# A graph network on one core: pre_u and pre_v from products of their own, and where VectorE's scoring stands in two units

## The chip, the cores and the metric

The kernel runs on one core of a Trainium2 chip. The metric is the device time of one launch in microseconds (us). The engines are TensorE (PE, with its weight loads shown as PEld), VectorE (DVE), ScalarE (ACT), GpSimd (POOL) and SyncE (SP). Each takes its own instructions in order. POOL and SP here mainly issue DMAs.

## The reference

64 graphs of 256 nodes with 256 features pass through four layers; `adj` (256x256, about 3% of its entries set, the same for all graphs) is shared. Three layers (L0, L1, L3) are alike; L2 is an attention layer.

```
pre_u = h @ W1[:d];  pre_v = h @ W1[d:]
hidden = relu(pre_u[:, :, None, :] + pre_v[:, None, :, :] + b1)
S   = sigmoid(hidden @ W2 + b2)              # one score for each edge (u, v)
a_t = einsum('buv,bud->bvd', S * A, h)
m_t = einsum('uv,bud->bvd', A, h) * h
z   = beta1*h + beta2*(a_t @ Wa + ba) + beta3*(m_t @ Wm + bm)
```

Scores are needed only where `adj` is not zero. All numbers are float32.

## The kernel before

**Pairs and units.** Graphs go two at a time (a pair, index g). Two pairs, side "a" and side "b", run interleaved. One round takes both pairs through all layers, and there are 16 rounds, written out one after another. A *unit* is the scoring of one side's pair in one of the layers L0, L1, L3, with the other side's remaining stages issued beside it. The order in a round is a/L0, b/L0, a/L1, b/L1, a/L3, b/L3. `beside(heavy, light, placed)` (L911) interleaves them: `heavy` is the scoring, `light` a generator of small steps that yields how many steps of scoring come next, a number for `made` or a pair for (`made`, `got`). `STEPS` (L45) and the list `beside` in `before` (L656) hold these numbers.

**Stages of a side.** `before(st, l)` (L646) computes pre_u and pre_v, adds b1, writes them to two DRAM tables, and prepares the first rows of `pre`. `scores` (L700) rates the edges, `spread` (L865) puts the scores into `sa`, and `finish` (L368) makes `a_t` and z. For L3 `attention` (L425) comes first. `mixed` (L334) makes `m_t`. In the pre_u/pre_v part, node blocks have the index m (128 nodes each).

**Scoring.** An edge block (128 edges, both graphs) is made in one of two ways. `made` picks rows with a matmul from `pre` into PSUM (`ga<-pre,pick`); the needed rows of `pre` are copied on ACT by `rows_u` and `rows_v`. `got` takes blocks that POOL has gathered from the tables by indirect DMA (`fetch`, L814): first u, then v added to it. A unit has 18 such DMAs (22 in b/L1 and a/L3): f = 0 to 7 (9), each with a u and a v part, and one "left" block (f = -1). In `FETCHES` the last five of 18 are v of f=4, u of 7, v of 5, v of 6, v of 7. All go through POOL's queue in order; the first AHEAD = 6 are issued within `before`, the others when the unit starts. DVE rates each block with two instructions (`junk<-ga`, `junk<-fetched`, one for each graph), which leave sums in `raw`. `rated_all` turns these into scores: ACT `val<-raw`, `val<-val`, and four DVE `rm<-gva,val`. EARLY covers the left block, the diagonal and all blocks of edge half m = 0 (f = 0 to 3 and made blocks 0 to 3), LATE (16 columns, at the end of a unit) those of m = 1. After EARLY comes `early` (L849): `ro` on ACT, PE `ps<-ro,guo`, four DVE `sa<-diag,val,ps`.

**The end of a unit.** `spread` is the first work of the next unit: 16 matmuls `ps<-rm,gu` (32 records in the trace) in two halves, m = 0 on EARLY's `rm` and m = 1 on LATE's, and a DVE `sa<-sa,ps` after each. The next unit's first `ga` matmul stands in their neighbourhood and needs `pre` row 0.

**Placed or not.** With `placed` true, `made`, the diagonal and the fetched blocks are held where the plan puts them (`stay` pins an instruction behind the last one of its engine), and EARLY comes in mid-unit after at least four made blocks. With `placed` false nothing is pinned, EARLY waits for all made blocks, and the framework's scheduler orders each engine's queue by readiness. Before, `placed` is true except beside the attention (b/L1, a/L3) and in the first and last unit: L892 gives true for L1, L893 false for L3, and L891 `i > 0` for both sides' L0; the flag comes from the light stream. So the b/L3 unit, beside a's last layer and a's next L0 `before`, has it true.

**pre_u and pre_v before** (L667 to L695). For each of the four (m, g) one 512-wide product writes u and v side by side into one PSUM bank; ACT copies the u half to `pu`, DVE adds b1 to the v half into `pv`. For L0 and L3 a third instruction adds u (from PSUM) and `pv` into `own`. After g = 1 of a block m the two table writes go to SP's queue, and after the one of m = 0 the first fetches. For L3 the order is g outer, because h of graph 1 is ready later. Two PSUM pools hold 5 banks (`ps`) and 3 banks (`ga`).

Of the kernel before, what the change touches and what calls it, by code (L numbers as in the profile page):

```python
# [12 lines left out]
ALU = mybir.AluOpType  # L13
AX = mybir.AxisListType

P = 128
B, N, D = 64, 256, 256
GNN = ("L0_gnn_", "L1_gnn_", "L3_gnn_")
LAST = GNN[2]
# [19 lines left out]
FETCHES = [(0, 0), (1, 0), (2, 0), (0, 1), (3, 0), (1, 1)]  # L39
FETCHES += [(-1, 0), (2, 1), (4, 0), (3, 1), (-1, 1), (5, 0), (6, 0), (4, 1), (7, 0), (5, 1), (6, 1), (7, 1)]  # L40
FETCHES_MORE = FETCHES[:-2] + [(8, 0), (6, 1), (9, 0), (7, 1), (8, 1), (9, 1)]
# [3 lines left out]
STEPS = {  # L45
    GNN[0]: [(1, 1), (1, 1), (0, 1), (1, 0), (0, 1), (2, 1)],
    GNN[1]: [0, 0, 0, (0, 1), (0, 1), 1],
    LAST: [1, (1, 1), 0, (1, 1), (0, 1), (2, 1)],
}

VEC = {}
# [11 lines left out]
def blk(c):  # L63
    return slice(c * P, (c + 1) * P)
# [37 lines left out]
def adj_seq_kernel(ctx: ExitStack, tc: tile.TileContext, a: dict, out: bass.AP):  # L102
# [187 lines left out]
    def stages(pools):  # L290
# [62 lines left out]
        def kept(st, l):  # L353

            hb = one.tile([P, 2, 2, N], FP, tag="hb", name="hb")
            for i in range(2):
                if l == LAST:
                    for m in range(2):
                        vector.scalar_tensor_tensor(
                            hb[:, i, m, :], st["h"][i][:, m, :], sca(l + "beta1"), zbrow, ALU.mult, ALU.add  # L360
                        )
                else:
                    scalar.activation(
                        hb[:, i], st["hT"][:, i], AF.Identity, bias=zbias[l][:, i : i + 1], scale=sca(l + "beta1")
                    )
            return hb

        def finish(st, l):  # L368

            sa, mT = st["sa"], st["mT"]  # L370
            hb = kept(st, l)
            aT = one.tile([P, 2, 2, N], FP, tag="aT", name="aT")
            for g in range(2):
                t = psum()
                product(t, st["h"][g], sa[:, :, g, :])
                scalar.copy(aT[:, :, g, :], t)
                yield STEPS[l][g]
            if l == LAST:
                for g in range(2):
                    z = psum()  # L380
                    for m in range(2):
                        for j, (w, y) in enumerate(((wm[l], mT), (wa[l], aT))):
                            for c in range(2):
                                mm(out=z[:, m, :], lhsT=y[:, c, g, blk(m)], rhs=w[:, c, :],
                                   start=j == 0 and c == 0, stop=j == 1 and c == 1)
                        yield STEPS[l][2 + 2 * g + m]
                    o = h_tile(st, g)
                    vector.tensor_tensor(o, hb[:, g], z, ALU.add)
                    nc.sync.dma_start(
                        out=of_graph(out, st["b"] + g), in_=o  # L390
                    )
                return
            hT = hT_tile(st)
            for m in range(2):
                z = psum()
                for j, (w, y) in enumerate(((wm[l], mT), (wa[l], aT))):
                    for c in range(2):
                        mm(out=z, lhsT=w[:, c, blk(m)], rhs=y[:, c], start=j == 0 and c == 0, stop=j == 1 and c == 1)
                    if j == 0:
                        yield STEPS[l][2 + 2 * m]  # L400
                vector.tensor_tensor(hT[:, m], hb[:, m], z, ALU.add)
                yield STEPS[l][3 + 2 * m]
            st["hT"] = hT
            st["h"] = []

            def turn(g):
                t = psum()
                flip(t, hT[:, :, g, :])
                h = h_tile(st, g)
                if l == GNN[1]:  # L410

                    vector.tensor_tensor(h, t, bias2.unsqueeze(1).to_broadcast([P, 2, D]), ALU.add)
                else:
                    scalar.copy(h, t)
                st["h"].append(h)

            if l == GNN[1]:
                for g in range(2):
                    turn(g)
                    yield 0  # L420
            else:

                st["turn"] = turn
# [78 lines left out]
    def few(stack):  # L502
# [139 lines left out]
        def more(st, l):  # L642

            return (st["side"], l) in (("a", LAST), ("b", GNN[1]))

        def before(st, l):  # L646

            hT = st["hT"]
            pu = one.tile([P, 2, 2, D], FP, tag="pu" + st["side"], name="pu")
            pv = one.tile([P, 2, 2, D], FP, tag="pv" + st["side"], name="pv")  # L650
            pre = one.tile([P, len(FAST), 2 * D], FP, tag="pre" + st["side"], name="pre")
            order = [(m, g) for m in range(2) for g in range(2)]
            if l == LAST:
                order = [(m, g) for g in range(2) for m in range(2)]

            beside = {LAST: [0, (0, 1), (0, 1), (0, 1)], GNN[1]: [0] + [(0, 1)] * 3, GNN[0]: [(0, 1)] * 4}[l]  # L656
            beside = dict(zip(order, beside))
            st["tables"] = [
                tables.tile([N, 2 * D], FP, tag="table" + t + st["side"], name="table" + t) for t in "uv"
            ]  # L660

            st["pu"], st["pv"], st["pre"] = pu, pv, pre
            if l != GNN[1]:
                st["own"] = one.tile([P, 2, 2, D], FP, tag="own", name="own")
            t = one.tile([P, FIRST, 2, D], FP, tag="fetched" + st["side"], name="fetched")
            st["fetched"] = [t[:, f] for f in range(FIRST)]
            for m, g in order:  # L667
                if l == LAST and (m, g) == (1, 0):
                    st["flip"](1)
                t = psum()  # L670
                for c in range(2):
                    mm(out=t, lhsT=hT[:, c, g, blk(m)], rhs=w1[l][:, c], start=c == 0, stop=c == 1)
                scalar.copy(pu[:, m, g, :], t[:, 0, :])
                vector.tensor_tensor(pv[:, m, g, :], t[:, 1, :], b1row[l], ALU.add)
                if g == 1:
                    for rows, x in zip(st["tables"], (pu, pv)):
                        nc.sync.dma_start(out=rows[blk(m)], in_=flat(x)[:, m])
                    if m == 0:
                        st["fetches"] = list(FETCHES_MORE if more(st, l) else FETCHES)

                        if numbered:
                            fetch(st, AHEAD)
                if l != GNN[1]:
                    vector.tensor_tensor(st["own"][:, m, g, :], t[:, 0, :], pv[:, m, g, :], ALU.add)
                if g == 1:
                    if m == 0:
                        rows_u(st, 0, 2, 0, 0)
                    rows_v(st, 4 - 4 * m, 2, 0)
                    st["rows"] = scalar.last.ins
                yield beside[(m, g)]  # L690
                if l == GNN[1] and (m, g) == (0, 1):
                    st["turn"](0)
                    yield 0, 1
                    st["turn"](1)
                    yield 0  # L695
            yield REST_OF_IT

            yield from mixed(st, l, later if past else None, (0,) if more(st, l) else (0, 1))
# [134 lines left out]
        def rows_u(st, f, n, k, m):  # L833

            h = halves[k]
            scalar.copy(
                st["pre"][h, f : f + n],
                st["pu"][h, m].rearrange("p g d -> p (g d)").unsqueeze(1).to_broadcast([64, n, 2 * D]),
            )

        def rows_v(st, f, n, k):

            for n in range(f, f + n):
                i = FAST[n][2]
                scalar.copy(
                    st["pre"][halves[1 - k], n], st["pv"][halves[i % 2], i // 2].rearrange("p g d -> p (g d)")
                )
# [37 lines left out]
        def stream(side, starts):  # L885

            sts = [{"b": b, "side": side} for b in starts]
            load(sts[0])
            short = [before(sts[0], GNN[0])]
            for i, st in enumerate(sts):  # L890
                yield short, (st, GNN[0]), i > 0  # L891
                yield [after(st, GNN[0]), before(st, GNN[1])], (st, GNN[1]), True  # L892
                yield [after(st, GNN[1]), attention(st), before(st, GNN[2])], (st, GNN[2]), False  # L893
                short = [after(st, GNN[2])]
                if i + 1 < len(sts):
                    load(sts[i + 1])
                    short = [halfway(after(st, GNN[2]), 4, before(sts[i + 1], GNN[0]), 2)]
            yield short, None, False
# [149 lines left out]
```

## Time and profile before

| what | us |
|---|---|
| median of 3 runs | 3446.23 (3439.92 to 3450.14) |
| profiled execution: time | 3460.79 |
| its span | 3459.1 |
| DVE busy | 2649.2 (77%) |
| ACT busy | 1555.9 (45%) |
| POOL busy | 2414.1 (70%) |

One round takes about 211 us of the span. The timeline from 1084.3 to 1295.1 us is such a round, beginning at the `spread` of a/L3: the six units from spread to spread take 30.90, 33.00, 32.10, 30.10, 41.20 and 43.50 us (b/L3, a/L0, b/L0, a/L1, b/L1, a/L3). A line of the timeline gives start, duration, engine, source line, operation, output and inputs, count, and in brackets the idle time of that engine before it with what ended it. All compute lines bear L79, that of a recording helper, so they are told apart by their tiles.

### The profile page before, as it was taken

The page shows a single profiled execution, that of the slowest core. Times are in us where ns is not written, and L with a number is a line of the kernel's source. Part 1 is how long each engine was busy: PE and PEld are TensorE (multiplying, and loading weights), DVE is VectorE, ACT ScalarE, POOL GpSimd, SP SyncE. Part 2 cuts the span into 40 slices and gives each one's busy share as a digit, 9 for nine tenths or more (in the row PEclk, how much of TensorE's full clock was granted, in tenths as well). Part 3 has the DMA queues.
Part 4 walks back from the last instruction along what each step waited for, and adds up shares of the span by engine and source line. Part 5 has one row for each costly group of instructions (what it writes and reads, how often), then busy time and mean ns, then how long its engine had stood idle before and what let it go on. Part 6 is the DMA issues. An engine that isn't in the chain of part 4 may idle for free.

```text
span 3459.1 us, 48323 instructions
## 1 busy us (share of the span) xinstructions
PE 3354.6 (97%) x14200; PEld 2069.3 (60%) x14200; DVE 2649.2 (77%) x10523; ACT 1555.9 (45%) x2833; POOL 2414.1 (70%) x1882
## 2 busy tenths in 40 slices
PE   6999999999999999999999999999999999999998
PEld 3566565666656566565665656656565665656655
DVE  5787787877778777777777877778787777777776
ACT  2444444444444444544444444444444444444442
POOL 3667777777767767677677776777767776776765
PEclk7999999999999999999999999999999999999999
DMA  5778787877878778788787877878787787887875
GB/s 152 159 185 190 166 207 166 194 177 176 198 167 195 179 179 187 168 190 181 170 190 174 201 169 187 188 165 206 164 194 179 176 195 172 194 181 179 193 163 123
DMA packets 289070, 620.81 MB, mean 179 GB/s; under 512 B 39072, under 2 KB 56352, under 8 KB 288800
## 3 DMA queue, kind: packets, MB, share of 16 engines
q0 software_dynamic: 204800, 461.49, 65.4%
q1 hardware_dynamic: 82416, 154.96, 12.8%
q8 instruction: 115, 1.88, 0.2%
q10 hardware_dynamic: 1584, 1.20, 0.1%
q14 instruction: 155, 1.27, 0.1%
HBM read 500.06 MB, written 117.44 MB: 179 GB/s over the span
## 4 chain that ended last, share of the span: by engine, by line
PE 80%; POOL 6%; DMA 5%; issue 4%; DVE 3%; ACT 2%; another core or an unknown queue 0%; ACTq 0%; POOLq 0%; SPq 0%; DVEq 0%
PE ps L79 62%; PE ga L79 17%; POOL fetched L827 5%; DMA fetched<-tablev,ids_v 3%; DVE junk L79 1%; DMA tableu<-pu 1%; ACT pre L79 1%; DVE sa L79 1%; POOL left L827 1%; DMA fetched<-tableu,ids_u 1%; ACT val L79 0%; ACT pu L79 0%; DVE rm L79 0%; ACT logits L79 0%; DVE scratch L79 0%
## 5 line engine op out<-in xcount | busy, mean ns | idle before, releaser
L827 POOL DMA_INDIRECT fetched<-tablev,ids_v x832 | 1319.8, 1586 | 365.9 <-issue 251.6
L827 POOL DMA_INDIRECT fetched<-tableu,ids_u x832 | 839.5, 1009 | 554.9 <-DMA tableu<-pu 292.7
L79 DVE SCALAR_TENSOR_TENSOR junk<-fetched,L_gnn_w2row 128x256 f32<-128x256 f32 x1664 | 639.0, 419 | 184.0 <-DMA fetched<-tablev,ids_v 179.5
L79 PE MATMUL ga<-pre,pick 128*128 128x512 f32 x1408 | 727.6, 611 | 28.4 <-ACT pre L79 16.0
L79 PE MATMUL ps<-L_gnn_w,hT 128*128 128x512 f32 x1536 | 706.9, 598 | 5.6 <-DMA hT<-in_xT_dram 5.6
L79 DVE SCALAR_TENSOR_TENSOR junk<-ga,L_gnn_w2row 128x256 f32<-128x256 f32 x1408 | 535.9, 419 | 92.0 <-PE ga L79 81.3
L79 PEld LDWEIGHTS ps<-L_gnn_w,hT 128*128 128x128 f32 x1536 | 280.0, 191 | 323.0 <-issue 297.5
L79 ACT COPY pre<-pv 64x512 f32<-64x512 f32 x704 | 434.1, 617 | 65.5 <-DVE pv L79 47.4
L79 PE MATMUL ps<-sa,h 128*128 128x256 f32 x1536 | 367.5, 384 | 25.0 <-DVE sa L79 18.2
L79 PEld LDWEIGHTS ps<-sa,h 128*128 128x128 f32 x1536 | 292.7, 192 | 141.9 <-issue 68.6
L79 ACT COPY pre<-pu 64x1024 f32<-64x1024 f32 x352 | 361.5, 1044 | 6.8 <-DVE ids_v L79 0.2
L79 ACT COPY pu<-ps 128x256 f32<-128x256 f32 x384 | 142.8, 372 | 471.5 <-PE ps L79 438.6
L79 PEld LDWEIGHTS ga<-pre,pick 128*128 128x128 f32 x1408 | 250.0, 191 | 171.6 <-issue 102.1
L79 DVE TENSOR_TENSOR rm<-gva,val 128x256 f32<-128x256 f32 x768 | 277.7, 420 | 60.5 <-ACT val L79 49.4
L79 PE MATMUL ps<-adj,h 128*128 128x256 f32 x1280 | 292.3, 379 | 1.3 <-issue 1.3
L79 PEld LDWEIGHTS ps<-adj,h 128*128 128x128 f32 x1280 | 243.4, 190 | 75.1 <-issue 40.9
L79 ACT ACTIVATE hb<-hT,L_gnn_zbias,scas 128x512 f32<-128x512 f32 x128 | 97.3, 806 | 414.5 <-DVE hT L79 370.2
L79 ACT COPY aT<-ps 128x512 f32<-128x512 f32 x192 | 112.3, 585 | 329.4 <-PE ps L79 320.5
L79 DVE TENSOR_TENSOR pv<-ps,L_gnn_b1row 128x256 f32<-128x256 f32 x384 | 161.7, 421 | 121.1 <-ACT pu L79 110.6
L79 PEld LDWEIGHTS ps<-rm,gu 128*64 128x64 f32 x3072 | 176.0, 137 | 121.1 <-issue 66.5
L79 PE MATMUL ps<-aT,L_gnn_Wa 128*128 128x512 f32 x512 | 240.6, 592 | 0.0
L79 PE MATMUL ps<-mT,L_gnn_Wm 128*128 128x512 f32 x512 | 240.6, 592 | 0.0
(149 smaller groups left out, 4183.4 us busy)
## 6 DMA issues: line engine op xcount, KB each, us to landing
tableu<-pu SPq DMA_DIRECT2D x192, 256.0 KB
tablev<-pv SPq DMA_DIRECT2D x192, 256.0 KB
hT<-in_xT_dram SPq DMA_DIRECT2D x32, 512.0 KB
h<-in_x_dram SPq DMA_DIRECT2D x64, 256.0 KB
out_dram<-h SPq DMA_DIRECT2D x64, 256.0 KB
fetched<-tableu,ids_u POOLq DMA_INDIRECT x832
fetched<-tablev,ids_v POOLq DMA_INDIRECT x832
L_gnn_w<-in_L_gnn_W_dram SPq DMA_DIRECT2D x6, 256.0 KB
```

The lines of the kernel that those rows point to most:

```text
L79: self.last = getattr(self.engine, op)(*a, **k)
L827: this = nc.gpsimd.indirect_dma_start(out=to, out_offset=None, in_=rows, in_offset=bass.IndirectOffsetOnAxis(ap=ids, axis=0), compute_op=( ...
```

## The change

Four things. (1) In `before` a product is now 256 wide and makes only u (n = 0, 2) or only v (n = 1, 3), for two graphs of one block m (L0, L1) or two blocks of one graph (L3); a bank holds u or v alone. ACT and DVE evacuate whole banks of 512. (2) `own` takes `pu` and `pv` from SBUF. (3) Table writes: for L0 and L1 each right after its product; for L3 both u writes after n = 2 and both v writes after n = 3. The first fetches follow n = 1 (L0, L1) or n = 3 (L3), and for L3 all four `rows_v` copies come after n = 3, those of rows 4 and 5 first. (4) The step plans of L3 and of a's L0 are changed, and `placed` for the unit beside a's L0 (b/L3) is false.

```diff
@@ STEPS
-    LAST: [1, (1, 1), 0, (1, 1), (0, 1), (2, 1)],
+    LAST + "a": [1, 1, (0, 1), (1, 1), (0, 1), (2, 1)],
+    LAST + "b": [1, (1, 1), 0, (1, 1), (0, 1), (2, 2)],
@@ finish
+            beside = STEPS[l + st["side"] if l == LAST else l]
...
-                yield STEPS[l][g]
+                yield beside[g]
@@ before
-            order = [(m, g) for m in range(2) for g in range(2)]
-            if l == LAST:
-                order = [(m, g) for g in range(2) for m in range(2)]
-
-            beside = {LAST: [0, (0, 1), (0, 1), (0, 1)], GNN[1]: [0] + [(0, 1)] * 3, GNN[0]: [(0, 1)] * 4}[l]
-            beside = dict(zip(order, beside))
+            beside = {LAST: [0, (0, 1), (0, 1), (0, 1)], GNN[1]: [0] + [(0, 1)] * 3, GNN[0]: [(0, 1)] * 4 if st["side"] == "b" else [0, 0, (0, 2), (0, 1)]}[l]
...
-            for m, g in order:
-                if l == LAST and (m, g) == (1, 0):
+            table = lambda x, m: nc.sync.dma_start(out=st["tables"][x][blk(m)], in_=flat((pu, pv)[x])[:, m])
+            for n in range(4):
+                i, x = n // 2, n % 2
+                mgs = [(m, i) for m in range(2)] if l == LAST else [(i, g) for g in range(2)]
+                part = lambda t: t[:, :, i, :] if l == LAST else t[:, i]
+                if l == LAST and n == 1:
                     st["flip"](1)
                 t = psum()
-                for c in range(2):
-                    mm(out=t, lhsT=hT[:, c, g, blk(m)], rhs=w1[l][:, c], start=c == 0, stop=c == 1)
-                scalar.copy(pu[:, m, g, :], t[:, 0, :])
-                vector.tensor_tensor(pv[:, m, g, :], t[:, 1, :], b1row[l], ALU.add)
-                if g == 1:
-                    for rows, x in zip(st["tables"], (pu, pv)):
-                        nc.sync.dma_start(out=rows[blk(m)], in_=flat(x)[:, m])
-                    if m == 0:
-                        st["fetches"] = list(FETCHES_MORE if more(st, l) else FETCHES)
-                        if numbered:
-                            fetch(st, AHEAD)
-                if l != GNN[1]:
-                    vector.tensor_tensor(st["own"][:, m, g, :], t[:, 0, :], pv[:, m, g, :], ALU.add)
-                if g == 1:
-                    if m == 0:
-                        rows_u(st, 0, 2, 0, 0)
-                    rows_v(st, 4 - 4 * m, 2, 0)
+                for j, (m, g) in enumerate(mgs):
+                    for c in range(2):
+                        mm(out=t[:, j, :], lhsT=hT[:, c, g, blk(m)], rhs=w1[l][:, c, x], start=c == 0, stop=c == 1)
+                if x == 0:
+                    scalar.copy(part(pu), t)
+                else:
+                    vector.tensor_tensor(part(pv), t, b1row[l].unsqueeze(1).to_broadcast([P, 2, D]), ALU.add)
+                if l != LAST:
+                    table(x, i)
+                elif i == 1:
+                    for m in range(2):
+                        table(x, m)
+                if n == (3 if l == LAST else 1):
+                    st["fetches"] = list(FETCHES_MORE if more(st, l) else FETCHES)
+                    if numbered:
+                        fetch(st, AHEAD)
+                if l != GNN[1] and x == 1:
+                    vector.tensor_tensor(*(part(t) for t in (st["own"], pu, pv)), ALU.add)
+                if n == (2 if l == LAST else 0):
+                    rows_u(st, 0, 2, 0, 0)
+                if x == 1 and l != LAST:
+                    rows_v(st, 4 - 4 * i, 2, 0)
+                elif n == 3:
+                    for f in (4, 0):
+                        rows_v(st, f, 2, 0)
+                if n == 3:
                     st["rows"] = scalar.last.ins
@@ stream
-                yield short, (st, GNN[0]), i > 0
+                yield short, (st, GNN[0]), i > 0 and side == "b"
```

More of the change, by code (lines that the diff above doesn't have):

```diff
@@ L385, in finish @@
                                    start=j == 0 and c == 0, stop=j == 1 and c == 1)
-                        yield STEPS[l][2 + 2 * g + m]
+                        yield beside[2 + 2 * g + m]
                     o = h_tile(st, g)
@@ L399, in finish @@
                     if j == 0:
-                        yield STEPS[l][2 + 2 * m]
+                        yield beside[2 + 2 * m]
                 vector.tensor_tensor(hT[:, m], hb[:, m], z, ALU.add)
-                yield STEPS[l][3 + 2 * m]
+                yield beside[3 + 2 * m]
             st["hT"] = hT
@@ L689, in before @@
+                if n == (2 if l == LAST else 0):
[6 more added lines that the diff above has]
+                if n == 3:
                     st["rows"] = scalar.last.ins
-                yield beside[(m, g)]
-                if l == GNN[1] and (m, g) == (0, 1):
+                yield beside[n]
@@ L692, in before @@
+                if l == GNN[1] and n == 1:
                     st["turn"](0)
```

## The prediction

> **What bounds the kernel now.** I read the page's busy shares first, then its chain, then for each unit the timeline around its end, engine by engine.
>
> ```profile
> PE 3354.6 (97%) x14200; PEld 2069.3 (60%) x14200; DVE 2649.2 (77%) x10523; ACT 1555.9 (45%) x2833; POOL 2414.1 (70%) x1882
> PE 80%; POOL 6%; DMA 5%; issue 4%; DVE 3%; ACT 2%; another core or an unknown queue 0%; ACTq 0%; POOLq 0%; SPq 0%; DVEq 0%
> ```
>
> PE is full, and its work does not shrink. Only its waits can. They sit at unit ends, where `spread` needs the last scores. The timelines of PE, DVE and POOL at the end of a b/L3 unit (`spread` of a/L3 at 1084.3 us, of b/L3 at 1115.2):
>
> ```profile
> 1115.20 1.09 PE L79 MATMUL ps<-rm,gu 128*64 128x128 f32 x16
> 1117.96 1.33 PE L79 MATMUL ps<-rm,gu 128*64 128x128 f32 x16 [1.67 <-DVE rm L79]
> ...
> 1115.31 0.43 DVE L79 SCALAR_TENSOR_TENSOR junk<-fetched,L_gnn_w2row 128x256 f32<-128x256 f32 x1 [0.91 <-DMA fetched<-tablev,ids_v]
> 1116.72 1.43 DVE L79 TENSOR_TENSOR rm<-gva,val 128x256 f32<-128x256 f32 x4 [0.63 <-ACT val L79]
> ...
> 1105.27 1.77 POOL L827 DMA_INDIRECT fetched<-tablev,ids_v  x1 [0.30 <-issue]
> 1107.35 1.79 POOL L827 DMA_INDIRECT fetched<-tablev,ids_v  x1 [0.30 <-issue]
> 1109.44 1.54 POOL L827 DMA_INDIRECT fetched<-tablev,ids_v  x1 [0.30 <-issue]
> ```
>
> The three POOL lines are v of f = 5, 6, 7. The last one ends at 1110.98; DVE gets its block at 1115.31, 4.33 us later, rates it (ends 1116.1), ACT makes the score, `rm` starts at 1116.72, and PE's second half follows 1.24 us after that, 1.67 us late. Over 15 rounds this half starts 33.7 us after the `spread` of a/L3 on average, as here (1117.96 - 1084.3).
>
> The other large wait is at the `spread` of b/L1 (ACT, DVE, PE):
>
> ```profile
> 1040.85 1.26 ACT L79 COPY pre<-pv 64x512 f32<-64x512 f32 x2
> ...
> 1040.28 0.42 DVE L79 TENSOR_TENSOR pv<-ps,L_gnn_b1row 128x256 f32<-128x256 f32 x1 [0.69 <-ACT pu L79]
> ...
> 1041.52 1.13 PE L79 MATMUL ga<-pre,pick 128*128 128x512 f32 x2 [1.29 <-ACT pre L79]
> 1042.58 1.63 PE L79 MATMUL ps<-rm,gu 128*64 128x128 f32 x25
> ```
>
> `spread` began at 1039.58, broke off, and PE waited 1.29 us for `pre` row 0, which needs the last `pv`, the last `val` and a copy. Mean over the rounds: about 1.1 us. At the ends of a/L0, b/L0 and a/L1, PE waits 0.1 to 0.5 us on average; at a/L3 the scores are 2 us early.
>
> **The change, part by part.**
>
> *Split products: +4.* 768 matmuls of 512 columns (1536 records, as PE passes each twice) become 3072 records of 256.
>
> ```profile
> 1004.51 3.62 PE L79 MATMUL ps<-sa,h 128*128 128x256 f32 x16
> 1007.96 1.88 PE L79 MATMUL ps<-mT,L_gnn_Wm 128*128 128x512 f32 x4
> 1009.68 1.88 PE L79 MATMUL ps<-aT,L_gnn_Wa 128*128 128x512 f32 x4
> ```
>
> Four wide records take 1009.68 - 1007.96 = 1.72 us, 430 ns each; 16 narrow ones, less the 384 ns that the last lasts, (3.62 - 0.38) / 15 = 216 ns. Two for one cost 1.5 to 3 ns (medians 429 and 216), 2 to 5 us in all. Loads double too; each narrow record above already has its own 192 ns load, inside 216 ns. [...]
>
> *Evacuation: 0.* Per unit, ACT's four 372 ns copies become two of 585; DVE's four `pv` of 421 become two like `sa<-sa,ps` 128x512 (685), likewise `own`. DVE's waits for ACT over one bank go:
>
> ```profile
> DVE pv L79 <- ACT pu L79: 110.6, 156, 1.1
> ```
>
> These 110.6 us stand in DVE's 23% idle; what they are worth is counted at the ends below. Were DVE full, they would be worth up to 110.6.
>
> *Earlier tables in L0 and L1: -3 at the ends of a/L0, b/L0, a/L1.* `tableu` of m = 0 now leaves one product (1.72 us) earlier, less the longer copy (0.21), so 1.5 us. POOL has waited for it before the first fetch of a/L1 and b/L1 by 4.3 and 3.5 us on average:
>
> ```profile
> POOL fetched L827 <- DMA tableu<-pu: 292.7, 61, 10.1
> ```
>
> So these two fetch chains move 1.5 us forward. a/L0 and b/L0 follow POOL's queue without a gap and gain nothing. Scores of a/L1 come 0.35 us sooner, where only four rounds in 16 waited, up to 0.4; bounds -8 and 0. For L3 both u writes stand ahead of the v writes in SP's queue, and the first u write leaves 0.2 us later; the 4th fetch is the first that needs v, three fetches of 1.3 us later, so nothing waits for v.
>
> *The `spread` of b/L1: -8.* In the built DVE queue, the fetched blocks 5 to 7 and `pv` of graph 0 now come first, then f = 8 (first graph), `own`, four `sa`, the rest of 8, 9, and the last `pv`. By the trace f = 8 lands 36.5 us after the previous `spread`; moved forward, 35.0, which in the unit above is 1035.4. Then 0.35 (block) + 0.6 + 1.57 + 1.04 + 0.65 brings the last `pv` to 1039.65, against 1040.7. But rows 4 and 5 now stand ahead of row 0 on ACT: three copies of 0.63, so row 0 at 1041.55, as before. What is gained is that 14 records of `rm,gu` run before the wait and not 6: 8 x 0.07 = 0.5 us x 16 = -8. If the fetches did not move, f = 8 costs 1.45 us: +14. If row 0 waited for nothing, -1.3 x 16 = -21.
>
> *b/L3 without placing: +25.* In the built DVE queue, EARLY's four `rm` now come after `left`, both halves of f = 4 and the first half of f = 5; then `pv`, the second half of 5, `own`, four `sa`, f = 6 and 7, two `hb`, then LATE's `rm`. DVE is strictly in order. By PE's pace it is ready for f = 5 about 24.9 us after the `spread` of a/L3. But f = 5 ends on POOL at 1107.04 and lands 4.0 to 4.3 us later: 26.8 in the mean of 15 rounds, plus 0.2 for the later table. Before, it was used at 29.1. So DVE idles 2 us, with the work behind it: 0.35 + 1.36 + 0.61 + 0.35 + 0.6 + 1.57 + 1.38 = 6.2 us. The last block ends at 27.1 + 6.2 = 33.3, two `hb` (0.85) end at 34.15, `rm` starts, and PE's second half comes 1.24 later: 35.4 against 33.7. +1.7 x 15 = +25 (the last b/L3 was never placed). PE itself gets there at 31.7. Late next is the m = 1 half of `sa`, then a's products. Lower bound: f = 5 in time, then the landing of f = 7 (30.5) sets the end, `rm` at 32.1, -0.4 x 15 = -6; upper: f = 5 one spread of its landings (1 us) later, +2.5 x 15 = +38. I take the mean landing. [...]
>
> **Sum** against the profiled execution (3460.8 around its span): +4 - 3 - 8 + 25 = +18, 3479. That execution lies 14.6 above the median, so the forecast is 3446 + 18 = **3464 us**. The bounds add to -33 and +57.
>
> **Rivals.**
>
> *Faster, 3425.* The mechanism is the fetch chain: if the block that b/L3's DVE meets first lands early, the stall does not arise (-6), and b/L1 loses its wait for row 0 (-21), with -8 and +4: -31 at best; I put it at -21. It decides if f = 5 lands within 25 us of the `spread`. For it: 18 fetches keep POOL at 1.6 us each and POOL waits 5 us before b/L3's first one. Against: that wait is for an L3 table, which does not come earlier.
>
> *No change, 3447.* b/L3 loses 0.8 and not 1.7 us (+12), and b/L1 gains as said. For it: landings scatter by 1 us, and PE's stall at `spread` already comes in some rounds and not in others.
>
> *Slower still, 3485.* ACT's row 0 becomes later: DVE waits for f = 8 as before (+14 in place of -8), b/L3 as forecast, +4 -3: +40.
>
> *The change doesn't do what it says:* excluded, as the built queues show the new order.
>
> **Chances.** Forecast 0.50, slower still 0.08, no change 0.20, faster 0.22. About 0.3% (10 us) is what a measurement of this kernel can tell from none; forecast and the still slower case lie beyond it, so slower 0.58, same 0.20, faster 0.22. The likeliest case alone spans 3452 to 3476. The range that leaves out a tenth at each side reaches into the faster case and the slowest one: 3420 to 3488.
>
> **What would show it.** Right: in b/L3 DVE idles about 2 us before a fetched block that stands ahead of EARLY's `rm`, and the second half of its `spread` waits over 3 us for `rm`; w1's narrow records at 216 ns; POOL's first fetch of a/L1 and b/L1 1.5 us earlier. Wrong: PE gaps between narrow records; f = 5 landing by 25 us; `ga` at b/L1's `spread` without a wait, or waiting 2.5 us and more.

## The result and the profile after

The changed kernel takes 3466.06 us (median of 6 runs, 3461.81 to 3470.07), the kernel before in the same session 3445.74 (3439.92 to 3450.2). The ratio is 1.0061, with a 95% interval from 1.0049 to 1.0074: 20 us slower. The profiled execution took 3468.59, its span 3466.9.

The page's busy shares and its chain after:

```profile
PE 3365.2 (97%) x15736; PEld 2367.9 (68%) x15736; DVE 2612.6 (75%) x10203; ACT 1525.3 (44%) x2641; POOL 2420.8 (70%) x1882
...
PE 60%; POOL 14%; DMA 11%; issue 7%; DVE 7%; ACT 1%; POOLq 0%; DVEq 0%; ACTq 0%
```

DVE and ACT have less to do (10203 and 2641 instructions in place of 10523 and 2833), yet the chain runs over POOL and the DMAs for 25% of the span, where it was 11%: it leaves PE at a wait and follows a fetch chain back. The waits of PE after:

```profile
PE ps L80 <- DVE rm L80: 44.8, 18, 5.6
PE ga L80 <- ACT pre L80: 17.1, 19, 1.7
```

The end of a b/L3 unit after, in the timelines of POOL, DVE and PE (`spread` of a/L3 at 1087.58, of b/L3 at 1118.67). The POOL line is v of f = 5:

```profile
1107.74 1.54 POOL L839 DMA_INDIRECT fetched<-tablev,ids_v  x1 [0.30 <-issue]
...
1114.03 0.42 DVE L80 SCALAR_TENSOR_TENSOR junk<-fetched,L_gnn_w2row 128x256 f32<-128x256 f32 x1 [1.77 <-DMA fetched<-tablev,ids_v]
1114.38 1.43 DVE L80 TENSOR_TENSOR rm<-gva,val 128x256 f32<-128x256 f32 x4
1115.72 0.68 DVE L80 TENSOR_TENSOR pv<-ps,L_gnn_b1row 128x512 f32<-128x512 f32 x1
...
1117.27 1.65 DVE L80 SCALAR_TENSOR_TENSOR sa<-diag,val,ps 128x256 f32<-128x256 f32 x4
...
1120.21 0.88 DVE L80 SCALAR_TENSOR_TENSOR hb<-h,scas,zbrow 128x256 f32<-128x256 f32 x2
1121.01 1.43 DVE L80 TENSOR_TENSOR rm<-gva,val 128x256 f32<-128x256 f32 x4
...
1118.67 1.09 PE L80 MATMUL ps<-rm,gu 128*64 128x128 f32 x16
1122.15 2.30 PE L80 MATMUL ps<-rm,gu 128*64 128x128 f32 x16 [2.38 <-DVE rm L80]
```

DVE idles 1.77 us before the first half of f = 5, which stands ahead of EARLY's `rm`, as forecast; LATE's `rm` follows 7 us later and PE waits 2.38 us (2.0 to 2.9 in the rounds; the prediction had asked for over 3). One number here was not forecast. The 16 records of the second half take 2.30 us; before the change they took 1.33, behind a wait of 1.67. The windows of the same unit, 3.41 us each (length, then busy time of PE, PEld, DVE, ACT and POOL with counts, granted clock, DMA share, GB/s):

```profile
1115.64:1119.05 3.41, 3.41 (x19) 2.39 (x19) 3.41 (x10) 1.23 (x2) 1.73 (x3) 1.00 0.97 282
1119.05:1122.47 3.42, 1.04 (x16) 0.66 (x12) 3.42 (x15) 2.07 (x4) 2.81 (x3) 1.00 0.75 170
1122.47:1125.88 3.41, 3.41 (x18) 2.40 (x17) 2.64 (x8) 3.34 (x5) 2.80 (x3) 0.50 0.71 137
```

In the second window PE is busy for 1.04 of 3.42 us, and in the third its granted clock is 0.50. So the wait is paid twice: as a wait, and as 3.41 us at half speed after it, which costs up to 1.7 us (3.41 x 0.5, an estimate). Between the start phase and the last unit the granted clock of this profile has 11 such stretches, one of them twice as long (12 x 3.41 us), all 3 to 6 us after the `spread` of b/L3. The first profile of the kernel before has 2, its second profile (below) has 1.

The lost time is best placed by the start of the second half (m = 1) of each `spread`, from one unit's to the next one's: means of rounds 1 to 14, in us. "Before" is the second profile of the kernel before, since the first one was disturbed (last experiment).

| second half of | before | after | difference | x 15 or 16 | forecast |
|---|---|---|---|---|---|
| a/L0 | 31.42 | 32.52 | +1.10 | +16 | a part of -3 |
| b/L0 | 31.98 | 31.75 | -0.23 | -4 | a part of -3 |
| a/L1 | 31.41 | 31.17 | -0.24 | -4 | a part of -3 |
| b/L1 | 40.18 | 39.64 | -0.54 | -9 | -8 |
| a/L3 | 41.79 | 42.52 | +0.73 | +12 | 0 |
| b/L3 | 32.81 | 33.99 | +1.18 | +18 | +25 |
| round | 209.59 | 211.59 | +2.00 | +29 | |

The two profiled spans differ by 28.5 us as well (3438.4 and 3466.9), the medians by 20. The +1.10 of a/L0 is the stretch at half clock, which lies behind b/L3's second half: in the four rounds without one this unit takes 31.32 us (before, most often 31.29), in those with one 32.6 to 33.0, and 34.03 behind the double one.

The +0.73 of a/L3 is a wait that the forecast lacked. ACT and PE at the end of an a/L3 unit after:

```profile
1083.99 0.31 ACT L80 ACTIVATE val<-raw,L_gnn_halfb 128x16 f32<-128x16 f32 x1 [2.40 <-DVE junk L80]
1084.60 2.51 ACT L80 COPY pre<-pv 64x512 f32<-64x512 f32 x4
...
1086.52 1.13 PE L80 MATMUL ga<-pre,pick 128*128 128x512 f32 x2 [1.45 <-ACT pre L80]
```

The four copies are rows 4, 5, 0, 1 of b's L3. Row 0 is the third, and b/L3's first `ga`, which stands ahead of a/L3's `spread`, waits 1.45 us for it. At this place PE waits in 13 of 16 rounds, 11.4 us in all; in the first profile of the kernel before it did not wait there at all, in the second 1.0 us.

At the `spread` of b/L1 the opposite happened. PE of the changed kernel there:

```profile
1042.90 1.09 PE L80 MATMUL ps<-rm,gu 128*64 128x128 f32 x14
1043.93 1.12 PE L80 MATMUL ga<-pre,pick 128*128 128x512 f32 x2
```

14 records of `rm,gu` stand ahead of the first `ga`, as forecast, in place of 6. But that `ga` waits in only four rounds of 16 (3.5 us in all); in the kernel before it waited in every round (16.0 us, in the second profile 10.7).

### The profile page after: what moved, and what is told of

It reads as the page before. It is cut to its first block, busy times and chain, and to the rows that moved or that the text cites. A ratio compares the mean times of both kernels' runs of the same rounds, so it can differ in the third digit from the quotient of the medians.

```text
span 3466.9 us, 50868 instructions
## 1 busy us (share of the span) xinstructions
PE 3365.2 (97%) x15736; PEld 2367.9 (68%) x15736; DVE 2612.6 (75%) x10203; ACT 1525.3 (44%) x2641; POOL 2420.8 (70%) x1882
## 4 chain that ended last, share of the span: by engine, by line
PE 60%; POOL 14%; DMA 11%; issue 7%; DVE 7%; ACT 1%; POOLq 0%; DVEq 0%; ACTq 0%
PE ps L80 46%; PE ga L80 14%; POOL fetched L839 12%; DMA fetched<-tablev,ids_v 7%; DVE junk L80 2%; DMA fetched<-tableu,ids_u 2%; POOL left L839 2%; DVE rm L80 1%; DVE sa L80 1%; ACT pre L80 1%; DMA tableu<-pu 1%; DVE pv L80 1%; DVE own L80 0%; DMA tablev<-pv 0%; DVE mT L80 0%
## 5 line engine op out<-in xcount | busy, mean ns | idle before, releaser
L80 DVE SCALAR_TENSOR_TENSOR junk<-fetched,L_gnn_w2row 128x256 f32<-128x256 f32 x1664 | 631.8, 420 | 191.4 <-DMA fetched<-tablev,ids_v 191.1
L80 PE MATMUL ps<-L_gnn_w,hT 128*128 128x256 f32 x3072 | 712.6, 382 | 5.6 <-DVE L_gnn_zb L80 5.6
L80 PEld LDWEIGHTS ps<-L_gnn_w,hT 128*128 128x128 f32 x3072 | 573.6, 191 | 136.6 <-issue 54.6
L80 PE MATMUL ps<-sa,h 128*128 128x256 f32 x1536 | 359.4, 380 | 0.0
L80 ACT COPY pu<-ps 128x512 f32<-128x512 f32 x192 | 112.6, 586 | 408.4 <-PE ps L80 403.0
L80 PE MATMUL ps<-rm,gu 128*64 128x128 f32 x3072 | 219.1, 285 | 44.9 <-DVE rm L80 44.8
```

The lines of the kernel that those rows point to most:

```text
L80: self.last = getattr(self.engine, op)(*a, **k)
```

## The experiments

Twelve more runs were made, each beside the kernel before. In the edits shown, `...` stands for lines left out. "Half clock" counts stretches of 3.41 us in the profile, start phase and last unit left out.

| kernel | median us | ratio to before, 95% | half clock |
|---|---|---|---|
| changed kernel | 3466.1 | 1.0061 (1.0049 to 1.0074) | 12 |
| f = 5 behind `rm` | 3436.6 | 0.9961 (0.9945 to 0.9977) | 5 |
| row 0 first | 3465.6 | 1.0052 (1.0033 to 1.0072) | 15 |
| placed as before | 3438.2 | 0.9974 (0.9961 to 0.9988) | 1 |
| fourth part alone | 3451.0 | 1.0008 (0.9995 to 1.0022) | 10 |
| added PE work | 3449.5 | 1.0013 (1.0002 to 1.0024) | 0 |
| split products alone | 3454.6 | 1.0022 (1.0011 to 1.0033) | 7 |
| f = 5 behind `rm`, row 0 first | 3442.9 | 0.9994 (0.9982 to 1.0007) | 8 |
| placed as before, u writes late | 3439.4 | 0.9980 (0.9971 to 0.9989) | 1 |
| f = 5 behind `rm`, added PE work | 3434.6 | 0.9964 (0.9950 to 0.9978) | 0 |
| placed as before, row 0 first | 3454.9 | 1.0025 (1.0010 to 1.0040) | 13 |
| placed as before, v before u | 3489.0 | 1.0125 (1.0105 to 1.0145) | 9 |
| the kernel before again | 3446.6 | 1.0006 (0.9990 to 1.0022) | 1 |

**Is it the place of f = 5?** One pin added to the changed kernel; `st["rm_last"]` is the last `rm` made so far, here EARLY's:

```diff
-                    with stay(vector):
+                    ahead = (st["side"], l) == ("b", LAST) and f == FIRST + 1
+                    with tc.issue_after(st["rm_last"].ins) if ahead else stay(vector):
...
```

> The changed kernel with one pin more: in b/L3 the block f = 5 stands in DVE's queue behind EARLY's last rm, as it stood by readiness in no round of the changed kernel. Theory (the in-order queue behind f = 5 sets b/L3's end): LATE's val comes about 31.2 us after the spread of a/L3 in place of 33.1, the second half of b/L3's spread and the first PE sa after it move back to where they were before (33.8 and 37.0 us in place of 34.9 and 39.3), and the time falls by 1.7 to 2.3 us x 15 = 25 to 34 us against the changed kernel, to about 3435. Rival (the loss is made elsewhere, at a/L3's ga or in PE's split products): DVE's wait for f = 5 changes place but the time stays within 6 us of the changed kernel's 3466. A second rival (the landing of f = 5 to 7 sets the end whatever the order): LATE's val moves less than 0.5 us.

Measured: 3436.6, 29.5 us under the changed kernel. DVE and PE at the end of a b/L3 unit of this version:

```profile
1106.87 1.43 DVE L80 TENSOR_TENSOR rm<-gva,val 128x256 f32<-128x256 f32 x4
...
1108.82 0.41 DVE L80 SCALAR_TENSOR_TENSOR junk<-fetched,L_gnn_w2row 128x256 f32<-128x256 f32 x1
...
1113.36 0.43 DVE L80 SCALAR_TENSOR_TENSOR junk<-fetched,L_gnn_w2row 128x256 f32<-128x256 f32 x1 [0.91 <-DMA fetched<-tablev,ids_v]
...
1115.94 1.42 PE L80 MATMUL ps<-rm,gu 128*64 128x128 f32 x16 [1.84 <-DVE rm L80]
```

`rm` no longer waits for f = 5 (it starts 25.0 us after the `spread` of a/L3, not 27.1), and DVE has next to no idle time before that block (0.07 us in the mean, 2.1 in the changed kernel). It now waits for f = 7 (the line at 1113.36). LATE's `val` comes at 32.0 us after the `spread` of a/L3, not at the expected 31.2, because f = 7 lands at 31.0; but the second half stands at 33.8 and PE's first `sa` at 37.5 (before 33.7 and 36.9, changed 34.9 and 39.3). Both rivals fall: the in-order queue behind f = 5 costs the time. Part of the 29.5 us is the clock again, since the shorter wait leaves 5 stretches at half clock where there were 12.

**The fourth part undone, and the fourth part alone.** In the first, `STEPS`, the list `beside` for L0 and `placed` are as before and all else is changed; in the second it is the other way round:

```diff
...
-                yield short, (st, GNN[0]), i > 0 and side == "b"
+                yield short, (st, GNN[0]), i > 0
```

> The changed kernel with its fourth part undone: b/L3 placed as before, the step plans of L3 and of a's L0 as before; split products, tables, evacuation and the order of the row copies stay changed. By the prediction's sum without its +25: -7 against the kernel before, about 3439, and 27 below the changed kernel. By what the two traces show (a/L3's ga waits 14 us that the prediction did not have): between -7 and +7 against before. Rival (the other three parts cost the time, not the placing): within 6 us of the changed kernel's 3466.

> The kernel before with the fourth part of the change alone: b/L3 not placed, and the new step plans; products, tables, evacuation and row copies as before. In its built queue for b/L3 EARLY's four rm stand ahead of f = 5, not behind it as in the changed kernel, so only some 4.25 us of DVE work stand behind that landing in place of 6.2. Theory (what costs is the place of f = 5 ahead of rm, which comes only of the four parts together): within -5 and +9 us of the kernel before. Rival (not placing costs by itself, wherever f = 5 stands): +20 to +34 against before, as in the changed kernel.

Measured: 3438.2 and 3451.0. Without its fourth part the change gains 9 us against the kernel before; the fourth part alone is within 0.22% of it. In that version EARLY's `rm` stands ahead of f = 5 in DVE's queue, so not placing b/L3 is not the cause by itself; the order that readiness gave it together with the other parts is. The flag and the step plans were not tried apart from each other.

By second halves the version with b/L3 placed takes 31.66, 32.02, 31.17, 39.50, 42.65 and 32.05 us, in the order of the table above. So its 9 us come at b/L3 (-0.76 a round), b/L1 (-0.68) and a/L1 (-0.24), against +0.86 at a/L3 and +0.24 at a/L0. a/L3 and b/L3 belong together: counted from the `spread` of a/L1, that of a/L3 stands where it stood (83.3 us, the wait for row 0 takes what b/L1 gained), but f = 7 of b/L3 lands 0.6 us earlier (113.6 and not 114.2), and b/L3 gets the time back.

**Is a part of it the clock?** If so, useless work for PE in the wait must make the kernel faster. For b/L3 the eight matmuls of the first half of `spread` are done three times over, into the same bank:

```diff
+                again = 3 if (st["side"], l, m) == ("b", LAST, 0) else 1
-                for i in range(4):
+                for i in list(range(4)) * again:
```

> The changed kernel with PE work added that does nothing new: in b/L3's spread the first half's eight matmuls for m = 0 are done three times over into the same bank, 32 records or about 1.75 us more, in the time in which PE waits for LATE's rm (2.3 to 3.2 us a round). Theory (a part of the loss is the granted clock): the changed kernel's profile has 12 stretches of 3.41 us at half clock within the rounds, 11 of them starting 3 to 5.6 us after b/L3's spread, where the kernel before has 2; 12 x 3.41 x 0.5 = 20 us at most. With PE kept busy in the wait these go, the wait itself stays: 14 to 21 us faster than the changed kernel, 3445 to 3452, with at most 3 such stretches left. Rival (only the wait counts, and the half clock lies beside other waits): within 5 us of 3466. Second rival (the added work is not hidden): slower, up to +26.

Measured: 3449.5, 16.5 us faster than the changed kernel, with 32 more records a round. PE's timeline and the window table of this version at the end of the same unit:

```profile
1115.31 2.84 PE L80 MATMUL ps<-rm,gu 128*64 128x128 f32 x48
1118.71 1.42 PE L80 MATMUL ps<-rm,gu 128*64 128x128 f32 x16 [0.56 <-DVE rm L80]
```

```profile
1115.64:1119.05 3.41, 2.85 (x48) 2.46 (x45) 3.41 (x15) 2.09 (x4) 2.41 (x2) 1.00 0.50 135
1119.05:1122.47 3.42, 3.42 (x22) 2.24 (x22) 3.42 (x10) 3.35 (x6) 2.81 (x3) 1.00 0.60 139
```

The second half still starts 3.4 us after the first (3.45 in the mean, 3.61 in the changed kernel), so the wait for LATE is nearly the same. But PE is busy in 2.85 of 3.41 us, no window at half clock follows, the second half takes 1.42 us, and the a/L0 unit takes 31.31 us in the mean in place of 32.52. Both rivals fall: about 16 us of the changed kernel's loss hang on the granted clock. They are not to be added to the 29.5 of the pin, which takes away part of the same half clock.

**The two edits together.** The pin and the repeated first half:

> The changed kernel with f = 5 of b/L3 behind EARLY's rm (3436.6 alone) and the first half of b/L3's spread done three times over, as in the run that added PE work. Theory (what is left after the first edit is half clock right after b/L3's spread, 5 stretches of 3.41 us in its profile): no such stretch left and 5 to 8 us faster than 3436.6, 3428 to 3432, so about 0.5% faster than the kernel before. Rival (in rounds where the wait is only 1.1 to 1.5 us the added 1.75 us of PE work comes out bare, up to 0.6 us x 15): within 3 us of 3436.6.

Measured: 3434.6 against 3436.6, ratios alike; the rival holds. No stretch at half clock is left, and PE's waits for `rm` fall from 30.4 to 5.4 us, but the added records come to 28 us (32 x 54 ns x 16) and cover waits of 1.1 to 2.8 us only in part. Either version is about 0.4% faster than the kernel before.

**Row 0 first**, in three versions: in the changed kernel, with the pin, and with b/L3 placed.

```diff
-                    for f in (4, 0):
+                    for f in (0, 4):
```

> The changed kernel with the two copies of L3's rows_v in the other order: row 0 first, rows 4 and 5 after it. Theory (row 0 as third copy on ACT makes PE's first ga wait at two places): the waits of ga for ACT's pre before the spread of a/L3 go (13.9 us in 16 rounds) and those of ga at b/L1's spread shrink by up to 0.6 us each (one copy of 0.63 us where two stood ahead; up to -10), so -14 to -24 against the changed kernel, 3442 to 3452. Rival (the wait only hides another one that ends next, rm at a/L3's spread): ga no longer waits, but the time stays within 5 us of 3466, and the waits of ps for rm grow by what ga lost.

> The changed kernel with f = 5 of b/L3 behind EARLY's rm and with row 0 first in L3's row copies. Alone, the first gave 3436.6 and the second 3465.6, no gain, though the waits of ga for ACT's pre fell from 17.1 to 8.6 us. Theory (b/L3's end is set by the landing of its fetch chain, f = 7 about 31 us after a/L3's spread, used 0.2 us later, so what is saved before it only makes that wait longer): within 5 us of 3436.6. Rival (f = 5 alone swallowed it): the 14 us come through, 3420 to 3427.

> The version with b/L3 placed as before (3438.2), with row 0 first in L3's row copies. Theory (b/L3's end hangs on the landing of f = 7, used 0.16 us later, so what a/L3's end gains is waited for there, and the longer wait of PE at b/L3's spread brings half clock): between 3434 and 3446, with more than the one stretch of half clock of that version. Rival (only f = 5 of the unplaced unit swallowed it): 14 us gained, 3420 to 3427.

Measured: 3465.6, 3442.9 and 3454.9, that is -0.5, +6.3 and +16.7 us against the same version without the edit. The expected 14 us come through in none, and two are slower beyond what I expected. PE's waits in the third, and in that version without the edit:

```profile
PE ps L80 <- DVE rm L80: 50.2, 20, 5.1
...
PE ga L80 <- ACT pre L80: 5.5, 8, 1.1
```

```profile
PE ps L80 <- DVE rm L80: 24.4, 18, 5.7
PE ga L80 <- ACT pre L80: 12.1, 19, 1.2
```

The short waits for row 0 go, and one longer wait at b/L3's `spread` takes their place. From second half to second half, b/L1 and a/L3 gain 0.48 and 0.45 us a round, b/L3 loses 2.04 and a/L0 1.34. The fetch chain did not move up with PE: f = 7 lands 2.0 us later after the `spread` of a/L3. The longer wait then brings half clock, 13 stretches in place of 1; 12 x 1.7 = 20 us at most. That b/L3 loses more than was gained ahead of it I can't explain: counted from the `spread` of a/L1 in both, its first fetch ends at about the same time (0.05 us later), v of f = 7 is issued 0.45 us later and lands 1.1 us later.

**The price of narrow records.** The kernel before with each product as two matmul pairs:

```diff
-                for c in range(2):
-                    mm(out=t, lhsT=hT[:, c, g, blk(m)], rhs=w1[l][:, c], start=c == 0, stop=c == 1)
+                for x in range(2):
+                    for c in range(2):
+                        mm(out=t[:, x, :], lhsT=hT[:, c, g, blk(m)], rhs=w1[l][:, c, x], start=c == 0, stop=c == 1)
```

> The kernel before with each product as two of 256 columns, u then v, into the same bank; nothing else is changed. Theory: 1536 records of 429 ns become 3072 of 216 ns, loads stay hidden: +2 to +5 us, so 0 to +8 against the kernel before with the scatter. Rival (PE shows gaps of the size of a weight load between narrow records): +50 us and more, with all 1536 added loads of 191 ns bare +293. [...]

Measured: a ratio of 1.0022 (0.11 to 0.33%), that is +7.6 us (+9.7 by the medians, 3454.62 and 3444.92). The groups of these records and their loads on the page of this version, and below them the kernel before:

```profile
L79 PE MATMUL ps<-L_gnn_w,hT 128*128 128x256 f32 x3072 | 712.5, 382 | 5.8 <-DMA hT<-in_xT_dram 5.8
...
L79 PEld LDWEIGHTS ps<-L_gnn_w,hT 128*128 128x128 f32 x3072 | 573.5, 191 | 136.8 <-issue 51.5
```

```profile
L79 PE MATMUL ps<-L_gnn_w,hT 128*128 128x512 f32 x1536 | 706.9, 598 | 5.6 <-DMA hT<-in_xT_dram 5.6
...
L79 PEld LDWEIGHTS ps<-L_gnn_w,hT 128*128 128x128 f32 x1536 | 280.0, 191 | 323.0 <-issue 297.5
```

PE's busy time grows by 5.6 us while the loads' grows by 293.5: the added loads are hidden, and the rival of +50 and more falls. The rest of the 7.6 may be clock: this profile has 7 stretches at half clock, the kernel before 1 or 2.

**What the earlier fetch chains are worth.** Two tries on the version with b/L3 placed. In the first both table writes of a block stand behind the v product again; in the second the products of L0 and L1 come as v, u, v, u, with `own` and `rows_u` after the u product:

```diff
-                if l != LAST:
-                    table(x, i)
+                if l != LAST and x == 1:
+                    table(0, i)
+                    table(1, i)
...
```

```diff
-                i, x = n // 2, n % 2
+                i, x = n // 2, n % 2 if l == LAST else 1 - n % 2
...
```

> The version with b/L3 placed as before (3438.2) with the u table writes of L0 and L1 put back behind the v product, the two of a block together. Theory (the gain of 9 us of the other three parts comes from fetch chains of a/L1 and b/L1 that start 1.5 us earlier): POOL's first fetch of a/L1 and b/L1 1.5 us later again, f = 8 of b/L1 landing at 35 and not 33.5 us, and +10 to +22 against 3438.2, so slower than the kernel before. Rival (the gain comes from the evacuation in whole banks, DVE no longer waiting for ACT): within 5 us of 3438.2.

> The version with b/L3 placed as before (3438.2), in L0 and L1 with the products in the order v, u, v, u in place of u, v, u, v, so that the u table of a block is written one product, 1.72 us, later. Theory of the prediction (the earlier u tables move the fetch chains of a/L1 and b/L1 forward, worth 3 us there and the greater part of b/L1's 8): POOL's first fetch of a/L1 and b/L1 1.5 us later, b/L1's f = 8 landing at 35 and not 33.6 us after the spread of a/L1, and +8 to +17, 3446 to 3455. Rival (what b/L1 gains is given back before the spread of a/L3, where ga waits for row 0 of pre): within 5 us of 3438.2.

Measured: 3439.4 and 3489.0. The first tells nothing of its question. POOL's first fetch of a/L1 and b/L1 stays where it was (5.65 and 3.90 us before the previous `spread`, against 5.87 and 3.89): SP issues the first u write 10.9 us before the `spread` that precedes a/L1 in both, wherever the write stands in the program. The second moves the chain, by more than meant: f = 8 of b/L1 lands at 36.4 and not 33.6 us, and b/L1 loses 3.24 us a round, a/L1 0.51. PE now waits 27.4 us in all for row 0 at the `spread` of b/L1 (1.5 in the version without the edit), and 8 of the 9 stretches at half clock stand behind it. The rival (within 5) falls, but the size, +51 where 8 to 17 were expected, need not be the chain's alone, since DVE gets a new wait whose share no run tells apart:

```profile
DVE own L80 <- ACT pu L80: 95.4, 77, 1.9
```

**The kernel before, profiled again.**

> The kernel before itself, for a second profile. In the first one the second sa<-sa,ps of a spread started 1 to 3 us late in some 25 of 96 units (DVE's waits put down to PE's ga, 31.8 us, and to a remote one, 7.2), which no profile of another version shows, and its execution lies 15 us above the median. Theory (a disturbance of that one execution, which made the base of the prediction's sum too high by about as much): no such waits now, a span within 6 us of 3444. Rival (it belongs to the old layout of the banks): the waits again, 20 us and more. Ratio 1 either way.

Measured: a span of 3438.4, and none of the late `sa`. DVE's waits at `sa<-sa,ps` in the first profile, and in the second:

```profile
DVE sa L79 <- PE ps L79: 49.5, 94, 3.0
DVE sa L79 <- PE ga L79: 31.8, 19, 2.7
DVE sa L79 <- remote: 7.2, 3, 2.9
```

```profile
DVE sa L79 <- PE ps L79: 24.8, 111, 0.9
```

So the execution on which the prediction's sum was made had a disturbance of its own. What it was stays open.

## Why the prediction was right

The forecast was +18 us to 3464; the kernel came to 3466. The cause it named is shown: undoing the fourth part gives 28 us back, pinning one block behind `rm` gives 29.5. That +18 and +20 lie so close is partly luck, as its terms show one by one:

- *Split products, +4.* Right in size by PE's busy time (+5.6); the version with nothing else changed came to +7.6.
- *Evacuation, 0.* DVE's waits for ACT at `pv` (110.6 us) are gone, as forecast, but DVE now waits there for the product itself (`pv` for PE `ps`, 135.5 us), so it did not get freer. The term was not tested by itself. It is contained in the 9 us that the first three parts gain together.
- *Earlier tables, -3.* POOL's first fetch of a/L1 and b/L1 moved by 1.45 and 1.49 us, as forecast. a/L1 gains 4 us, also in the version with b/L3 placed (31.17 there too), so the term is about right. The 4 us of b/L0 are not of it: with b/L3 placed that unit takes 32.02 us, with the fourth part alone 31.71. The forecast put the term down to the earlier product and the longer copy, which holds; the place of the write in the program has no part in it.
- *The `spread` of b/L1, -8.* Measured -9. 14 records stand ahead of the first `ga`, as forecast, but row 0 was to come too late for it all the same, with f = 8 landing at 35.0. f = 8 lands at 33.5, and in 12 of 16 rounds the wait is gone. The prediction had named a `ga` without a wait here as a sign of being wrong: the size is right, the wait that was to remain is not there.
- *a/L3, nothing.* Wrong, +12. The prediction saw that rows 4 and 5 stand ahead of row 0 on ACT and costed it at b/L1 alone; of a/L3 it said that the scores are 2 us early, and did not ask what else the first `ga` there needs. With this wait what b/L1 gained is given back at once. With row 0 first, 4.0 of its 11.4 us are left.
- *b/L3, +25.* f = 5 lands 26.7 us after the `spread` of a/L3 (forecast 27.1) and DVE idles 2.1 us (forecast 2). But the second half starts at 34.9 and not at 35.4: DVE takes up f = 5 0.35 us earlier than forecast, and the steps behind it take 0.15 us less. That makes +18 in place of +25. This error hangs together with the one before: the wait for row 0 holds up the `spread` of a/L3, from which all this is counted, and not the fetches (with row 0 first this `spread` comes 1.0 us earlier after that of a/L1, f = 7 only 0.2). In the changed kernel with row 0 first, f = 5 lands at 27.2 and the second half starts at 35.5, as forecast, and the time is the same.
- *Not in the sum: the granted clock.* Up to 12 x 1.7 us; without these stretches the kernel is 16.5 us faster. The prediction took a wait of PE to cost what it lasts.

From the forecast's +18 to the table's +29: +12 (a/L3), +16 (half clock, in a/L0), -7 (b/L3), -5 (b/L0 and a/L1), -1 (b/L1), and -4 for the split products, which the table has inside its units. From +29 to the 20 between the medians it is the two profiled executions, one 6 us under its median and one 2.5 above. So the total came nearer than its terms deserved: the cause was right and so were the signs of the two large terms, but a wait and the clock were missing (+28), and smaller terms (-17) and the scatter of the executions (-9) took most of it back.

One aside of the prediction does not come out of its own numbers: its case of no change adds to +12 - 8 - 3 + 4 = +5, that is 3451 and not 3447. The landing that it took from the trace held: v of f = 5 lands 4.4 us after its issue ends (mean of 15 rounds after the change), where the forecast had 4.0 to 4.3.

## What to carry to other kernels

Where a scheduler orders an in-order engine by readiness, look for the block that needs a late transfer and for what stands behind it: moving one block was worth 0.85% here. A wait of PE can cost more than its length: half clock followed 11 of the changed kernel's 15 waits at b/L3's `spread`, and PE work put into them took 16.5 us off the time. One long wait can cost more than several short ones: the edit that traded the latter for the former gave -0.5, +6.3 and +16.7 us in three versions (row 0 first). Ask at each place where an input is reordered who else reads it first.

## What the runs showed of the hardware

The stretches at half clock in the changed kernel's profile and in the first one of the kernel before, start phase and last unit left out, last 3.413 us each, one of them 6.827; within a profile they start whole multiples of 3.413 us apart. Cut into windows of that length, from the first stretch on, the two profiles show this (PE's busy time is that of the window tables above):

| windows at full clock | changed kernel | half clock next | kernel before | half clock next |
|---|---|---|---|---|
| PE busy for under 1.7 us of 3.41 | 11 (0.55 to 1.63 us) | 11 | 7 (1.26 to 1.68 us) | 2 |
| PE busy for longer | 939 (from 1.92 us) | 0 | 951 (from 1.73 us) | 0 |

The two of the kernel before have 1.26 and 1.51 us, the five without half clock behind them 1.46 to 1.68.

The length of a wait alone did not decide this. In the changed kernel PE paused for 2.3 to 3.2 us (from start to start of the records) between the halves of b/L3's `spread`, and half clock followed in 11 of 15 rounds: not in one with a pause of 3.16 us, but in one with 2.31. In the four rounds without it this `spread` starts 0.87 to 1.61 us into a window; in the eleven with it at 0.17 and 0.41 (one each), at 1.21 (one) and from 2.55 to 3.21 us (eight). Six of the ten steps between the changed kernel's stretches are 211.63 us, which is 62 windows, and its round takes 211.59 us in the mean. In the last five of the 15 rounds the `spread` of b/L3 starts within 0.5 us of one place in the window and half clock follows each time; in the earlier ones the place wanders. In the kernel before a round takes 209.6 to 210.8 us (two profiles). That the length of the round itself adds to the loss is not shown.
